# Attention products with V issued for two key steps at a time, seven weight tiles, and the biases loaded later

## The chip, the cores and the metric

One NeuronCore of a Trainium2 chip runs the kernel. The metric is the device time of one execution in microseconds; the time before is the median of three runs. Engines are called PE (TensorE, matrix products), PEld (its weight loads, which overlap PE), DVE (VectorE), ACT (ScalarE), POOL (GpSimd) and SP (the queue that issues the transfers). PSUM has 8 banks of 128 x 512 f32, into which PE writes.

## What is computed

A transformer block on x of 16 x 1024 x 256, f32. Both halves read the layer-normed x, and their results are added to x.

```python
x = L0_attn_x                                     # (16, 1024, 256)
xn = _layernorm(x, axis=-1)
x = x + _L0_attn_ref(xn, ...) + _L0_ffn_ref(xn, ...)

# attention: 16 heads of 16, rotary positions, causal
Q, K, V = x @ Wq.T + bq, x @ Wk.T + bk, x @ Wv.T + bv
scores = einsum('bhqd,bhkd->bhqk', rope(Q), rope(K)) / 4, masked to keys <= query
out = einsum('bhqk,bhkd->bhqd', softmax(scores), V) @ Wo.T + bo

# feed-forward: squared relu, then five steps of a threshold neuron, counted
h = square(relu(x @ W_fc.T)); y = h @ W_proj.T    # 1024 hidden
mem = 0.9 * mem + y - (mem > 1); count += (mem > 1)   # 5 times, count / 5
```

## The kernel before

**Arithmetic.** A full-width product is done as three f16 products of high and low parts (`three`, L599), 128 x 128 weights with 256 or 512 columns. Scores have 16 rows a head, and with the parts of the split they have 48 to 50; two such products lie in the upper and the lower half of the array's rows. The products with V have f32 operands, 17 of 32 columns of the array for each of four heads, so that four lie side by side. The code calls these three layouts of the array FULL, ROWS and COLS.

**Units.** A batch has four units of four heads, 64 units in all. For each unit, `largest` (scores at L797) finds the rows' maxima with DVE (L813, L831), turns them with a small COLS product (L858) and writes them into the operand `qS` by DMA. `weighted` then does the same scores transposed (L914), with the maxima taken off in the product; ACT takes the exponential out of the bank into a tile `w` (L975), 128 keys x 2 heads x 512 queries; POOL zeroes the part past the diagonal (L932); PE multiplies by V (L941) into a bank `pav` in which all key steps of 512 queries add up. There are two blocks of 512 queries; the first has 3 steps of keys, the second 7. A step has four exponentials in two tiles `w`, and one op with its products with V: 4 heads x 1 part, or x 2 parts where two narrow diagonal parts share a step. An f32 product is two instructions in the trace, so a step of one part is 8 matmuls at L941. At the last step, `avT` is copied out and goes through DRAM to be divided by the sums (`av`, `inv`, `ahl`), and `projected` applies Wo.

**Beside it.** `forward` does the feed-forward: `ph` (12 products), relu and squares in a tile `relu`, split into `hT`, then `py` (12 products) and five threshold counts. `norms`, `rotated` (Q and K, bias, rotation in tiles `qk` and `ms`, split into `qkhl`, stored to DRAM `scr_q`, `scr_k`, read back by `load_slots` as `qS`, `kS`) and `values` prepare the next batch. For batch 0, DVE does the rotation; for the others POOL does it.

**Order.** Nothing is ordered by hand. Each piece of work is an `op` with an engine, a cost and a due time; `Plan.order` plays the whole kernel forward with these costs and writes down the order in which each engine starts its ops, and that order is fixed in the program. An op may start at most WINDOW (93 us of the plan's time) before it is due. Tiles come from rings (`BUFS`: the number of buffers for each name), and an op isn't taken until its tiles and banks are free in the plan. Banks are shared out by kind (`CAPS`). PE prefers work in the layout that it is in, and a change costs SWITCH = 100 ns in the plan. In this version the plan's costs are also varied by up to 3%, with a seed for each stretch of 70 us (`DRAWN`, `VARIED`).

**Start.** SP first issues x, Wqkv, cos and sin. `load_small` (L534 to L537, five transfers: Wo in two, bv in two of 128 single elements each, bo) follows, then the transposes of the normed x (L636), which PE's first full products wait for. A small product of bv and Wo (L555) adds the bias of V to bo; x times 5 plus that bias (L1144, L1146) is prepared for each pair of row blocks.

## Time and profile before

| what | value |
|---|---|
| median of 3 runs (lowest to highest) | 2427.77 us (2427.6 to 2428.23) |
| the profiled execution, its own time | 2432.1 us |
| its span, first to last instruction | 2430.4 us |
| DVE busy | 2000.4 us (82%) |
| ACT busy | 1878.6 us (77%) |
| POOL busy | 1769.9 us (73%) |
| exponentials (L975, ACT) | 2560, 1246.4 us |
| products with V (L941, PE) | 6144 matmuls, busy 620.7 us |
| scores (L914 and L797, PE) | 3072 matmuls each, busy 430.5 and 420.6 us |
| full products (L599, PE), the two largest groups | 379.8 and 353.5 us busy |
| mean granted PE clock | 0.992 |

A row of a group gives the line, engine, operation and tile, how many there are, the busy time and the mean duration in ns; a row of the timeline gives its start, how long it lasts until the last of its merged instructions ends, and their number. Matmuls overlap in the pipeline, so their busy time is longer than the distance from start to start, and the starts are what a sum over PE's work goes by. A wait is listed as waiter <- releaser: total us, times, longest.

### The profile page before, as it was taken

To read this page: it belongs to the slowest core of one execution; us is meant where nothing else is said; L and a number is where in the kernel's file an instruction comes from. 1 tells how busy PE (TensorE), PEld (TensorE's weight loads), DVE (VectorE), ACT (ScalarE), POOL (GpSimd) and SP (SyncE) were. 2 spreads that over 40 slices of the span, in tenths; PEclk is the share of its full clock that TensorE was granted. 3 is DMA by queue.
4 is the path that set the end of the run, shared out by engine and by line. 5 is a ranking of instruction groups with operands and counts; after the bars stand their busy time and mean duration, and the time that the engine had idled before them with its cause. 6 is when DMAs were issued, how large, how long until landed. Compare 5 with 4: busy or idle time off the path is not lost. (4 is left out here: it accounts for less than half of the span.)

```text
span 2430.4 us, 58976 instructions
## 1 busy us (share of the span) xinstructions
PE 2344.1 (96%) x20996; PEld 1175.5 (48%) x20996; DVE 2000.4 (82%) x6070; ACT 1878.6 (77%) x3671; POOL 1769.9 (73%) x1897
## 2 busy tenths in 40 slices
PE   4999999999999999999999999999999999999997
PEld 2644444454455444454544445445454444545453
DVE  7788888888978888878888887988878888787982
ACT  5588788877877877878778877777877878778774
POOL 4878778777787787768768687676876858787453
PEclk9999999999999999999999999999999999999998
DMA  7443533524334243244342334333433343433221
GB/s 180 107 104 85 137 85 102 133 80 111 94 106 120 86 120 106 85 107 118 90 120 87 100 115 102 98 91 93 117 92 100 103 108 95 106 107 88 65 59 50
DMA packets 253936, 246.22 MB, mean 101 GB/s; under 512 B 108104, under 2 KB 207816, under 8 KB 253640
## 3 DMA queue, kind: packets, MB, share of 16 engines
q1 hardware_dynamic: 253504, 242.44, 36.4%
q8 instruction: 165, 2.70, 0.5%
q14 instruction: 131, 1.07, 0.2%
q10 hardware_dynamic: 136, 0.00, 0.0%
HBM read 122.82 MB, written 101.71 MB: 92 GB/s over the span
## 5 line engine op out<-in xcount | busy, mean ns | idle before, releaser
L975 ACT ACTIVATE w<-banks 128x512 f32<-128x512 f32 (+1 forms) x2560 | 1246.4, 573 | 285.3 <-PE banks L914 267.3
L813 DVE TENSOR_REDUCE nm_sb<-banks 128x1 f32<-128x512 f32 x1024 | 643.3, 682 | 138.8 <-PE banks L797 134.6
L941 PE MATMUL banks<-w,v_sb 128*32 128x512 f32 (+3 forms) x6144 | 620.7, 495 | 2.4 <-POOL w L932 0.4
L932 POOL TENSOR_SCALAR_AFFINE_SELECT w<-w 128x256 f32<-128x256 f32 x1024 | 398.0, 407 | 287.2 <-ACT w L975 275.1
L831 DVE CUSTOM_DVE_ANT_0 junk<-banks,mask,nm_sb 128x256 bf16<-128x256 f32 (+3 forms) x1024 | 498.7, 546 | 71.6 <-PE banks L797 40.2
L831 DVE CUSTOM_DVE_ANT_0 junk<-banks,mask 128x256 bf16<-128x256 f32 (+3 forms) x1024 | 444.6, 486 | 75.7 <-PE banks L797 60.3
L914 PE MATMUL banks<-qS,kS 50*128 50x512 f16 (+3 forms) x3072 | 430.5, 327 | 12.3 <-DVE nm_sb L831 7.6
L797 PE MATMUL banks<-kS,qS 48*128 48x512 f16 (+3 forms) x3072 | 420.6, 326 | 14.2 <-DVE nm_sb L831 5.4
L599 PE MATMUL banks<-wproj_hi,hT 128*128 128x256 f16 x2048 | 379.8, 274 | 1.1 <-DVE nm_sb L831 0.6
L599 PE MATMUL banks<-xT,wfc_hi 128*128 128x256 f16 x2048 | 353.5, 275 | 6.5 <-ACT qk L679 2.3
L599 PEld LDWEIGHTS <-hT 128*128 128x128 f16 x3072 | 281.0, 98 | 105.3 <-issue 73.7
L1113 POOL TENSOR_TENSOR relu<-relu 128x1024 f32<-128x1024 f32 x111 | 211.1, 1902 | 160.6 <-ACT hT L1111 160.3
L599 PE MATMUL banks<-xT,wfc_lo 128*128 128x256 f16 x1024 | 280.4, 274 | 0.0
L599 PE MATMUL banks<-wproj_lo,hT 128*128 128x256 f16 x1024 | 279.4, 273 | 0.0
L1117 POOL TENSOR_TENSOR hT<-relu,hT 128x1024 f16<-128x1024 f32 x128 | 274.1, 2141 | 3.6 <-ACT relu L1115 1.7
L914 PEld LDWEIGHTS <-kS 50*128 50x128 f16 x3072 | 132.9, 94 | 296.3 <-issue 269.1
L797 PEld LDWEIGHTS <-qS 48*128 48x128 f16 x3072 | 138.7, 94 | 277.7 <-issue 236.1
L941 PEld LDWEIGHTS banks<-w,v_sb 128*32 128x32 f32 x6144 | 151.6, 108 | 250.8 <-issue 195.3
L1128 DVE SCALAR_TENSOR_TENSOR x<-banks,x 128x512 f32<-128x512 f32 x320 | 219.0, 684 | 46.0 <-PE banks L599 39.1
L1106 ACT ACTIVATE relu<-banks 128x512 f32<-128x512 f32 x256 | 156.3, 611 | 121.6 <-PE banks L599 118.2
L599 PEld LDWEIGHTS <-wfc_hi 128*128 128x128 f16 x2048 | 184.6, 98 | 95.2 <-issue 72.7
L686 POOL TENSOR_TENSOR ms<-qk,sin_sb 128x1024 f32<-128x1024 f32 x60 | 142.0, 2367 | 47.6 <-ACT qk L679 47.6
(81 smaller groups left out, 2798.5 us busy)
## 6 DMA issues: line engine op xcount, KB each, us to landing
av_dram<-avT SPq DMA_DIRECT2D x128, 256.0 KB, 2.5
qS<-scr_q SPq DMA_DIRECT2D x128, 192.0 KB, 3.6
kS<-scr_k SPq DMA_DIRECT2D x128, 192.0 KB, 4.4
x<-in_x_dram SPq DMA_DIRECT2D x66, 256.0 KB, 3.7
scr_q<-qkhl SPq DMA_DIRECT2D x32, 512.0 KB, 3.1
scr_k<-qkhl SPq DMA_DIRECT2D x32, 512.0 KB, 3.1
av<-av_dram SPq DMA_DIRECT2D x64, 256.0 KB, 3.4
inv<-inv SPq DMA_DIRECT2D x64, 256.0 KB, 3.4
```

The costliest lines, as they stand in the source:

```text
L599: nc.tensor.matmul(out, lhsT=lhs[i], rhs=rhs[j], start=first and n == 0, stop=last and n == 2)
L797: nc.tensor.matmul(pts[two].t[:, at : at + w], lhsT=qS.t[r, h, c * P : (c + 1) * P], rhs=kS[r, h, k0 : k0 + w], start=True, stop=True,)
L813: lambda two=two, pt=pt: nc.vector.tensor_reduce(nm0[:, two, i, c : c + 1], pt.t, axis=AX.X, op=ALU.max),
L831: nc.vector.tensor_tensor_reduce(next(junk)[:, :w], pt.t[:, at : at + w], mask[:, QB - w :], scale=1.0, scalar=nm0[:, two, i, chunk] if pa ...
L914: nc.tensor.matmul(pts[two].t[:, at : at + n], lhsT=kS[r, i, j * P : (j + 1) * P], rhs=qS.t[r, i, qb * QB + off : (qb + 1) * QB], start=Tr ...
L932: nc.gpsimd.affine_select(out=d, in_=d, compare_op=ALU.is_ge, fill=0.0, base=0, pattern=[[0, 2], [1, P]], channel_multiplier=-1,)
L941: nc.tensor.matmul(pav.t[VT * h : VT * (h + 1), off:], lhsT=st.v[:, j, col : col + VT], rhs=ws[h % 2].t[:, h // 2, at : at + QB - off], st ...
L975: lambda n=n, two=two, pt=pt, w=w: nc.scalar.activation(w.t[:, two, :n], pt.t[:, :n], AF.Exp, scale=SCALE),
L1106: lambda r=r, ph=ph, pr=pr: nc.scalar.activation(r.t[:, 2 * pr : 2 * pr + 2].rearrange("p f t -> p (f t)"), ph.t, AF.Relu, scale=1.0 / WS),
L1113: combined(1024, when + 4e3, lambda e, r=r: e.tensor_tensor(r.t, r.t, r.t, ALU.mult), [], [(r, 0), (r, 1)], 1.75, lambda r=r: nc.scalar.ac ...
L1117: lambda e, r=r, hT=hT: e.tensor_tensor(hT.t[:, 1], r.t, hT.t[:, 0], ALU.subtract),
L1128: nc.vector.scalar_tensor_tensor(xc, py.t, WS * LEAST[step], xc, ALU.is_gt, ALU.add)
```

## The change

The products with V are collected (`given`) and issued as one op for two steps of keys (JOINED = 2), or for what is left at the last step of a block of queries. The ring `w` has seven tiles instead of five; for the space, `x` has eight instead of nine and `ahl` five instead of six, and the rotation's tile `ms` has no ring of its own any more but takes a buffer of the two in the ring `relu`. The due time of a product is 12 us after its step instead of 8 (LAG). `load_small` is due at 32 us of the plan's time instead of -20 us, and the loads of x for batch 0's result may not start much before it. The variation of the plan's costs is gone.

```diff
-LAG = 8e3
+LAG = 12e3
-BUFS = dict(w=5, xn=2, x=9, relu=2, hT=3, avT=2, ahl=6)
+BUFS = dict(w=7, xn=2, x=8, relu=2, hT=3, avT=2, ahl=5)
+JOINED = 2
-SMALL = -20e3
+SMALL = 32e3
-VARIED, STRETCH = 0.03, BATCH / 2
-DRAWN = [
...
-                    cost *= varied.uniform(1 - VARIED, 1 + VARIED)
...
-    op("sp", dma(5), SMALL, load_small, [], ["small", wo_stage], size=1400.0, window=10e3)
+    op("sp", 5e3, SMALL, load_small, [], ["small", wo_stage], size=1400.0, window=10e3)
...
-                ms = held("ms", 1, [P, 2, QB], F32, f"ms_{b}_{t}_{half}")
+                ms = held("relu", 2, [P, 2, QB], F32, f"ms_{b}_{t}_{half}")
...
-        def product(pav, ws, parts, first, last):
-            for n, (qb, j, off, at) in enumerate(parts):
+        def product(pav, given, first, last):
+
+            todo = [(ws, part) for ws, parts in given for part in parts]
+            for n, (ws, (qb, j, off, at)) in enumerate(todo):
                 for h in range(4):
...
-                        start=first and n == 0, stop=last and n == len(parts) - 1,
+                        start=first and n == 0, stop=last and n == len(todo) - 1,
...
-                pav = bank(f"pav_{unit}_{qb}")
+                pav, given, begun = bank(f"pav_{unit}_{qb}"), [], True
...
-            op("pe", pe(n, 4) + 20 * len(parts), when + LAG,
-               lambda pav=pav, ws=ws, parts=parts, first=first, last=last: product(
-                   pav, ws, parts, first, last),
...
+            given = given + [(ws, parts)]
+            if len(given) == JOINED or last:
+                all_parts = [part for _, parts in given for part in parts]
+                op("pe", sum(pe(QB - part[2], 4) + 20 for part in all_parts), when + LAG,
+                   lambda pav=pav, given=given, begun=begun, last=last: product(pav, given, begun, last),
+                   [*[(w, two) for ws, _ in given for w in ws for two in range(2)],
+                    *[(key, st.b % 2, part[1] // 2) for part in all_parts for key in ("v", "v taken")]],
+                   [pav], mode=COLS)
+                given, begun = [], False
...
-                        st.x[t - 1] = x_ = load_x(b, t - 1, "x", times[0] - 15e3)
+                        st.x[t - 1] = x_ = load_x(
+                            b, t - 1, "x", times[0] - 15e3,
+                            min(WINDOW, times[0] - 5e3 - SMALL) if b == 0 else None)
```

More of the change, by code (lines that the diff above doesn't have):

```diff
@@ L3 @@
 from itertools import cycle
-from random import Random
 import numpy as np
@@ L219, in order @@
         mode = None
-        drawn, change, varied = list(DRAWN), -1e9, None
         def turn(t, need):
@@ L273, in order @@
             now = events[0][0]
-            if now >= change:
-                varied = Random(drawn.pop(0) if drawn else 0)
-                change = S0 + STRETCH if change < S0 else change + STRETCH
             while events and events[0][0] <= now:
@@ L424, in held, with load_x @@
         return Held(sb, tag, BUFS.get(tag, bufs), shape, dtype, name)
-    def load_x(b, n, tag, when):
+    def load_x(b, n, tag, when, window=None):
         t = held(tag, 0, [P, 2, D], F32, f"{tag}_{b}_{n}")
         op("sp", 500, when, lambda: nc.sync.dma_start(t.t, tokens(x, b, n)), [], [t],
-           size=move(P * 2 * D * 4))
+           size=move(P * 2 * D * 4), window=window)
         return t
@@ L981, in weighted @@
                        [(w, 0), (w, 1)])
-            op("pe", pe(n, 4) + 20 * len(parts), when + LAG,
-               lambda pav=pav, ws=ws, parts=parts, first=first, last=last: product(
-                   pav, ws, parts, first, last),
-               [*[(w, two) for w in ws for two in range(2)], *[(key, st.b % 2, part[1] // 2) for part in parts for key in ("v", "v taken")]], [pav], mode=COLS)
+            given = given + [(ws, parts)]
[7 more added lines that the diff above has]
+                given, begun = [], False
             if last:
```

2 lines of the change are left out of this document (removed).

## Prediction

> **What bounds the kernel now.** I read the busy shares first, then the waits, then the timeline of PE.
>
> ```profile
> PE 2344.1 (96%) x20996; PEld 1175.5 (48%) x20996; DVE 2000.4 (82%) x6070; ACT 1878.6 (77%) x3671; POOL 1769.9 (73%) x1897
> ```
>
> PE is the bound, and it is idle for little. The list of waits agrees: ACT and POOL wait for hundreds of us, PE's longest entries are a few us each.
>
> ```profile
> ACT w L975 <- PE banks L914: 267.3, 288, 4.0
> PE banks L599 <- ACT qk L679: 8.5, 3, 6.2
> PE banks L914 <- DVE nm_sb L831: 7.6, 13, 3.1
> ```
>
> So time comes off only where PE's own steps get shorter or its small waits do. What a step costs stands in PE's timeline, in the starts. Three cuts from it: a lone step of products with V, a doubled one (which this order already has in places), and a change between full and row layout.
>
> ```profile
> 412.02 0.60 PE L914 MATMUL banks<-qS,kS 50*128 50x512 f16 x4
> 412.56 1.06 PE L941 MATMUL banks<-w,v_sb 128*32 128x512 f32 x8
> 413.56 0.39 PE L797 MATMUL banks<-kS,qS 48*128 48x512 f16 x2
> ...
> 878.20 0.60 PE L797 MATMUL banks<-kS,qS 48*128 48x384 f16 x6
> 878.73 1.92 PE L941 MATMUL banks<-w,v_sb 128*32 128x512 f32 x16
> 880.59 0.61 PE L914 MATMUL banks<-qS,kS 50*128 50x512 f16 x4
> ...
> 401.68 0.27 PE L599 MATMUL banks<-wo_lo,ahl 128*128 128x256 f16 x1
> 401.78 0.27 PE L599 MATMUL banks<-wo_hi,ahl 128*128 128x256 f16 x1
> 401.99 0.39 PE L914 MATMUL banks<-qS,kS 50*128 50x384 f16 x4
> 402.22 0.38 PE L797 MATMUL banks<-kS,qS 48*128 48x512 f16 x2
> ```
>
> From the start of L941 to the next scores, 8 matmuls take 413.56 - 412.56 = 1.00 us and 16 take 880.59 - 878.73 = 1.86, so a second step costs 0.86 and entering and leaving the layout the rest. With the way in (scores to L941 takes 0.31 as the median of the trace, scores to scores 0.22) a lone excursion costs 0.31 + 1.00 - 0.22 = 1.09; less the 0.86 of its work, 0.23 us go to two changes of layout, 0.11 each. Full to row is 401.99 - 401.78 = 0.21 where full to full is 0.10 to 0.11: 0.10 for that change.
>
> **Joined products: the sum.** In the built order, 640 products with V become 384 ops; runs of PE's order in one layout fall from 2367 to 2053, so 314 changes are saved. The column layout is entered 358 times instead of 578, full against row changes rise from 1210 to 1336. That is 440 changes saved at 0.11 (48 us) less 126 added at 0.10 (13 us): -35 us. More exactly, I gave every succession of two PE steps its median start-to-start gap in the trace and added these along both orders: 2277.6 us before, 2244.8 after. **I take -33 us**; the count of changes alone bounds it at -30 to -36. It lies on the path, PE's own queue.
>
> From its first to its last matmul PE takes 2402.3 us, so 124.7 us are waits and the slower clock: 23 up to 125 us, 82 up to 2385, 19 in the tail. These can grow.
>
> **Joined products: the waits.** An op waits for eight exponentials and their masks instead of four, and holds four of seven tiles `w` meanwhile (two of five before). Behind it in PE's queue stand scores, and ACT waits for those. I added the same medians of the PE work that stands between the last scores of a step and its product: in the worst tenth 2.07 us before, 2.06 after. Between a bank's scores and its next use, for scores after exponentials: 1.31 before and 1.62 after. The cover is no thinner, so I take the middle stretch at -4 us, pro rata to 6% fewer PE ops; bounds: -10, and +15, a fifth more waits, if the order made from unvaried costs meets ACT and DVE less well.
>
> **Two bare stretches.** The new order has two places without full products between the attention steps, where PE can only follow ACT. The row for such a place is the last stretch before:
>
> ```profile
> 2385.00:2409.00 24.00, 21.98 (x177) 8.42 (x174) 3.81 (x6) 18.61 (x41) 8.71 (x18) 0.93 0.13 36
> ...
> L975 ACT ACTIVATE w<-banks 128x512 f32<-128x512 f32 (+1 forms) x38 | 17.6, 575 | 4.1 <-PE banks L914 4.1
> ```
>
> (Columns: stretch, length, PE, PEld, DVE, ACT, POOL, granted clock, DMA share, GB/s.) 38 exponentials in 24 us are 0.63 us each; ACT's own work bounds it below at 17.6/38 = 0.46.
> First, the tail: the last `py` now ends 33 us of PE work before the end, with 66 exponentials to go (18 us and 37 before). 66 x 0.46 = 30 to 66 x 0.63 = 42 us against 27.5 us of PE work up to the last projection: +3 to +14, less the 6 that the old tail loses by the same count. I take +5, bounds -3 to +9. The chain after it (store, sums, `inv`, `ahl`, projection) is the same.
> Second, near 300 us, where batch 3 is prepared: 23 us of PE work with 44 exponentials and two `pv`, no `ph`, no `py`. Its four `ms` now take the two `relu` buffers in turn, each held through three POOL passes of 2.37, 2.37 and 2.55 us, and `ph` can't start without one. ACT's other work there is 10 us (3 `qkhl`, 2 `qk`, 2 `avT`, the norm of four row blocks, by their rows 3.2 + 1.4 + 1.2 + 3.9). 44 x 0.46 + 10 is 30 us, 44 x 0.63 is 28 without it and 38 with it: +5 to +15; **I take +9**.
> The clock: 0.93 over 24 us is 1.7 us lost there, so +2 for the two (0 to +5).
>
> [...]
>
> **Seven tiles, rings, costs.** The tiles change no instruction. x at eight and `ahl` at five have rings that the order was built with; the projection's cover over its `ahl` stays 39 us in the middle (40 before). Seven relu squares move from ACT to POOL, 7 x 1.9 = 13 us on an engine busy 73%. Nothing, covered by PE; uncovered at most 13, as far as it falls in the bare stretch and is counted there.
>
> **The biases.** Before, SP issues them ahead of the first transpose:
>
> ```profile
> 8.79 0.60 SPq L534 DMA_DIRECT2D wo_stage<-in_wo_dram  x1
> ...
> 15.89 0.54 SPq L535 DMA_DIRECT2D bv_sb<-in_bv_dram  x1
> 19.55 0.35 SPq L537 DMA_DIRECT2D bo_sb<-in_bo_dram  x1
> ...
> 21.53 1.37 SPq L636 DMA_TRANSPOSE xT<-xhl  x1
> ```
>
> The normed tile that it turns is done at 14.6 us (DVE L658), so PE's first full product, 4.1 us behind the transpose at 25.6, can start at 18.7: 6.9 us sooner. But PE's first scores wait for batch 0's keys, which come through DVE's rotation, a store and a load:
>
> ```profile
> PE banks L797 <- DMA kS<-scr_k: 1.5, 1, 1.5
> ```
>
> They start at 79.9, 13.2 us after DVE's last rotation op ended (66.7), 54.3 us behind the first full product; 37.9 of those are PE work. In the new order 30.5 us of PE work stand there, and DVE has 1.7 us more in the chain (the bias ops). So scores start at 18.7 + 54.3 + 1.7 = 74.7, with 7.4 us less work done: 5.2 sooner by the clock, 2.2 lost by the work. The five transfers stand now ahead of the first store of Q, which waits for DVE until about 40; they need 12.7 us from about 26 on and are covered. Not covered, they would delay that store. I take 0; bounds -7 (the chain isn't late) and +3.
>
> **Sum.** 2430.4 - 33 - 4 + 5 + 9 + 2 + 0 = 2409 us of span. The profiled execution has 1.7 us around its span and stands 4.3 over the median, so its span is 2.6 over: 2409 - 2.6 = **2406 us**.
>
> **The rivals.**
> - *The bare stretches cost nothing and the early start is kept.* For it: ACT is busy only 77%, and it could run at its 0.46 there. Against: the row of 0.63. 2427.8 - 33 - 4 - 7 = 2384.
> - *No change.* Joined waits eat the saving: 384 ops, each late by 0.09 us, make 33. For it: PE's weight loads wait for POOL's masks in 79 places already (28 us). Against: the covers above. 2427.
> - *Slower: the shared ring.* `ms` and `relu` meet in every batch, not only where the order shows a bare stretch; if `ph` is late on the chip at each preparation, a stretch like the one at 300 us stands in the others too. At 9 us each it decides from the fourth on (4 x 9 > 33). With six: 2406 + 5 x 9 = 2451. For it: POOL waits up to 13 us for ACT at L1113, so the relu chain is often late. Against: the order has full products between the scores everywhere else, and each `relu` is 25 us ahead of its `py`.
> - *It doesn't join*, because the order doubled products already: excluded by the 358 against 578 runs.
>
> **Chances.** Forecast 0.62, first rival 0.20, no change 0.08, slower 0.10. A measurement here tells 0.2%, 5 us, from no change. Faster: 0.82, same 0.08, slower 0.10. The bounds of the unknown costs seldom all fall one way; their distances from the values taken, squared and added, give -13 to +21, so 2393 to 2427 for the forecast alone. The range reaches down to 2384 for the first rival and ends at 2426; left out are the slower case, half of no change and some 0.06 of the first rival, 0.2 in all.
>
> **What would show it.** Right: L941's runs of 8 mostly gone in PE's timeline and a lone excursion again at 1.00; PE's first full product near 18.7 us; scores' wait for `kS` of several us where 1.5 stood; PE idle near 300 us and in a tail of about 40 us behind the last `py`; PE's busy time lower by about the overlap of the changes. Wrong: PE waits on `w` all through, POOL masks as releasers of L941 grown beyond 28 us, or bare stretches at other batches.

## The result, and the profile after

The changed kernel takes 2446.79 us (median of 6 runs, 2442.22 to 2456.57), the kernel before 2428.0 beside it (6 runs, 2426.13 to 2433.61). The ratio is 1.0074, with a 95% interval of 1.0058 to 1.009: slower by 19 us, where 2406 was forecast. The profiled execution took 2446.82 us, its span is 2445.1. The one before, of 2430.4, stood 4 us over its median, so the two spans differ by 14.7 only. Line numbers are 8 to 10 lower than before: full-layout products are L589, scores for the maxima L787, scores for the exponentials L904, products with V L933, exponentials L967, the reductions of the maxima L803 and L821.

The busy shares of the page, which the prediction read first:

```profile
PE 2328.7 (95%) x20996; PEld 1205.1 (49%) x20996; DVE 1985.7 (81%) x6068; ACT 1866.8 (76%) x3666; POOL 1782.0 (73%) x1904
```

PE does the same 20996 matmuls and is busy 15.4 us less, and yet the span is 14.7 us longer: what PE saved, and as much again, has become waiting. PE's timeline says that its steps are what the change wanted (columns: start, us from the first start to the last end, engine, line, operation, tiles, shape, count):

```profile
999.67 1.04 PE L933 MATMUL banks<-w,v_sb 128*32 128x512 f32 x8
1000.64 0.39 PE L787 MATMUL banks<-kS,qS 48*128 48x512 f16 x2
...
1003.56 1.93 PE L933 MATMUL banks<-w,v_sb 128*32 128x512 f32 x16
1005.42 0.61 PE L787 MATMUL banks<-kS,qS 48*128 48x512 f16 x6
```

A lone step takes 1000.64 - 999.67 = 0.97 us to the next start (1.00 before), a joined one 1005.42 - 1003.56 = 1.86 (1.86). The list of waits (engine and line, what it waited for; us in total, times, longest):

```profile
ACT w L967 <- PE banks L904: 226.6, 236, 3.2
...
ACT avT L396 <- PE banks L933: 121.9, 76, 4.5
...
PE banks L589 <- DMA xT<-xhl: 21.9, 2, 19.1
PE banks L589 <- DVE nm_sb L821: 11.5, 32, 1.0
...
PE banks L904 <- DVE nm_sb L821: 8.6, 22, 1.3
PE banks L787 <- DVE nm_sb L821: 7.7, 20, 0.9
PE banks L589 <- ACT qk L669: 6.1, 6, 4.7
```

The third line is PE's start: its first full product now stands at 19.09 us. The lines with `nm_sb` are PE waiting for a bank that VectorE's maxima still hold: L589, L904 and L787 together 27.8 us in 74 times. The same three entries before (the one of L914 stands in the prediction) sum to 16.6 us in 39:

```profile
PE banks L797 <- DVE nm_sb L831: 5.4, 13, 1.8
PE banks L599 <- DVE nm_sb L831: 3.6, 13, 0.4
```

SP's queue, for the biases:

```profile
14.81 1.36 SPq L626 DMA_TRANSPOSE xT<-xhl  x1
...
27.77 0.62 SPq L524 DMA_DIRECT2D wo_stage<-in_wo_dram  x1
28.45 0.58 SPq L525 DMA_DIRECT2D bv_sb<-in_bv_dram  x1
```

The first transpose stands at 14.81 (21.53 before), the biases behind it. Now the two stretches without full-layout products, by windows (columns as in the prediction; the eighth figure, before the DMA share, is the granted clock):

```profile
352.00:397.00 45.00, 39.76 (x301) 14.61 (x299) 33.62 (x116) 32.71 (x69) 37.09 (x42) 0.85 0.40 111
...
2370.00:2385.00 15.00, 12.56 (x110) 3.98 (x110) 14.93 (x43) 10.21 (x20) 2.84 (x3) 1.00 0.10 37
...
2385.00:2400.00 15.00, 12.93 (x78) 3.79 (x80) 1.49 (x6) 9.80 (x24) 6.09 (x15) 0.70 0.06 20
2400.00:2415.00 15.00, 12.60 (x70) 2.86 (x62) 0.35 (x1) 9.52 (x19) 0.81 (x2) 0.73 0.17 55
```

Before, the first stretch of the tail was

```profile
2360.00:2385.00 25.00, 24.25 (x224) 12.18 (x223) 16.77 (x48) 18.84 (x37) 14.20 (x15) 1.00 0.10 34
```

The tail now has two halves. Up to 2385 VectorE is busy 14.93 of 15 us (16.77 of 25 before), most of it with the maxima: they bound it. Behind that no engine is busy throughout: PE is busy 12.93 and 12.60 of 15, ScalarE 9.80 and 9.52, at a granted clock of 0.70 and 0.73 (0.93 in the tail before). In the rows of the timeline a bracket gives the idle time before and what ended it. One turn of it, from the timeline:

```profile
2402.05 5.01 ACT L967 ACTIVATE w<-banks 128x512 f32<-128x512 f32 x10
...
2405.67 3.06 PE L933 MATMUL banks<-w,v_sb 128*32 128x512 f32 x16
...
2408.66 0.61 PE L904 MATMUL banks<-qS,kS 50*128 50x512 f16 x4
2409.15 3.04 ACT L967 ACTIVATE w<-banks 128x512 f32<-128x512 f32 x6 [2.08 <-PE banks L904]
```

A joined product that took 1.93 us in the middle takes 3.06 here. ScalarE runs out of filled score banks meanwhile and idles for 2.08 us, until PE has issued scores again.

Laid out as in the prediction, for three kernels (the last is the first experiment below). "PE sum" is the sum of the median gaps of before along each order; "excess" is what PE's starts took beyond it, in waits and at half clock.

| us | before | changed | changed, products single |
|---|---|---|---|
| first matmul | 23.75 | 19.09 | 17.72 |
| PE sum | 2277.6 | 2244.8 | 2280.1 |
| excess up to 125 us | 23.4 | 27.8 | 27.5 |
| excess 350 to 400 us | 2.0 | 17.7 | 6.5 |
| excess from 2340 us | 20.5 | 39.8 | 21.9 |
| excess elsewhere | 78.9 | 91.6 | 85.2 |
| behind the last matmul's start | 4.3 | 4.3 | 4.1 |
| span | 2430.4 | 2445.1 | 2443.0 |

The PE sum fell by 32.8 us and the start came 4.7 earlier; 52.1 us of excess took the place of these.

### The profile page after: what moved, and what is told of

It is laid out like the page before. It is cut to its first block, busy times and chain, and to the rows that moved or that the text cites. A ratio compares the mean times of both kernels' runs of the same rounds, so it can differ in the third digit from the quotient of the medians.

```text
span 2445.1 us, 58685 instructions
## 1 busy us (share of the span) xinstructions
PE 2328.7 (95%) x20996; PEld 1205.1 (49%) x20996; DVE 1985.7 (81%) x6068; ACT 1866.8 (76%) x3666; POOL 1782.0 (73%) x1904
## 4 chain that ended last, share of the span: by engine, by line
PE 62%; DVE 19%; ACT 7%; issue 5%; DMA 4%; POOL 3%; SPq 1%; DVEq 0%; POOLq 0%; ACTq 0%
PE banks L589 29%; PE banks L933 16%; PE banks L904 9%; PE banks L787 8%; DVE junk L821 7%; DVE nm_sb L803 5%; ACT w L967 5%; DVE x L1125 3%; DVE nm_sb L821 1%; DVE stats L606 1%; PE banks L848 1%; DMA x<-in_x_dram 1%; DMA qS<-rows 1%; DMA inv<-inv 1%; DMA xn<-in_x_dram 1%
## 5 line engine op out<-in xcount | busy, mean ns | idle before, releaser
L967 ACT ACTIVATE w<-banks 128x512 f32<-128x512 f32 (+1 forms) x2560 | 1248.5, 578 | 245.8 <-PE banks L904 226.6
L803 DVE TENSOR_REDUCE nm_sb<-banks 128x1 f32<-128x512 f32 x1024 | 641.2, 682 | 149.0 <-PE banks L787 148.1
L821 DVE CUSTOM_DVE_ANT_0 junk<-banks,mask,nm_sb 128x256 bf16<-128x256 f32 (+3 forms) x1024 | 498.1, 546 | 98.8 <-PE banks L787 67.6
L933 PE MATMUL banks<-w,v_sb 128*32 128x512 f32 (+3 forms) x6144 | 569.8, 499 | 6.6 <-DVE nm_sb L803 2.0
L821 DVE CUSTOM_DVE_ANT_0 junk<-banks,mask 128x256 bf16<-128x256 f32 (+3 forms) x1024 | 445.6, 486 | 82.7 <-PE banks L787 64.7
L904 PE MATMUL banks<-qS,kS 50*128 50x512 f16 (+3 forms) x3072 | 437.8, 328 | 21.5 <-DVE nm_sb L821 8.6
L787 PE MATMUL banks<-kS,qS 48*128 48x512 f16 (+3 forms) x3072 | 411.8, 326 | 13.6 <-DVE nm_sb L821 7.7
L589 PE MATMUL banks<-wproj_hi,hT 128*128 128x256 f16 x2048 | 380.3, 274 | 3.9 <-DVE nm_sb L821 2.8
L589 PE MATMUL banks<-xT,wfc_hi 128*128 128x256 f16 x2048 | 352.0, 274 | 16.1 <-DVE nm_sb L821 4.8
L589 PEld LDWEIGHTS <-hT 128*128 128x128 f16 x3072 | 282.2, 98 | 107.1 <-issue 76.0
L933 PEld LDWEIGHTS banks<-w,v_sb 128*32 128x32 f32 x6144 | 172.3, 111 | 316.8 <-issue 258.9
L1110 POOL TENSOR_TENSOR relu<-relu 128x1024 f32<-128x1024 f32 x118 | 223.5, 1894 | 122.1 <-ACT hT L1108 122.0
L589 PE MATMUL banks<-wproj_lo,hT 128*128 128x256 f16 x1024 | 279.8, 273 | 0.0
L589 PE MATMUL banks<-xT,wfc_lo 128*128 128x256 f16 x1024 | 279.8, 273 | 0.0
L904 PEld LDWEIGHTS <-kS 50*128 50x128 f16 x3072 | 133.5, 94 | 261.4 <-issue 231.3
L787 PEld LDWEIGHTS <-qS 48*128 48x128 f16 x3072 | 139.4, 94 | 221.2 <-issue 172.5
L589 PEld LDWEIGHTS <-wfc_hi 128*128 128x128 f16 x2048 | 186.0, 98 | 105.7 <-issue 85.0
L1125 DVE SCALAR_TENSOR_TENSOR x<-banks,x 128x512 f32<-128x512 f32 x320 | 217.8, 681 | 23.4 <-PE banks L589 16.5
L821 DVE DVE_READ_ACCUMULATOR2_ANT nm_sb<- 128x1 f32 x2048 | 168.7, 82 | 0.0
```

What stands on the lines that cost most here:

```text
L589: nc.tensor.matmul(out, lhsT=lhs[i], rhs=rhs[j], start=first and n == 0, stop=last and n == 2)
L787: nc.tensor.matmul(pts[two].t[:, at : at + w], lhsT=qS.t[r, h, c * P : (c + 1) * P], rhs=kS[r, h, k0 : k0 + w], start=True, stop=True,)
L803: lambda two=two, pt=pt: nc.vector.tensor_reduce(nm0[:, two, i, c : c + 1], pt.t, axis=AX.X, op=ALU.max),
L821: nc.vector.tensor_tensor_reduce(next(junk)[:, :w], pt.t[:, at : at + w], mask[:, QB - w :], scale=1.0, scalar=nm0[:, two, i, chunk] if pa ...
L904: nc.tensor.matmul(pts[two].t[:, at : at + n], lhsT=kS[r, i, j * P : (j + 1) * P], rhs=qS.t[r, i, qb * QB + off : (qb + 1) * QB], start=Tr ...
L933: nc.tensor.matmul(pav.t[VT * h : VT * (h + 1), off:], lhsT=st.v[:, j, col : col + VT], rhs=ws[h % 2].t[:, h // 2, at : at + QB - off], st ...
```

## The experiments

Three theories went in. *Bare stretches*: where no full-layout product is left to put between the attention's steps, PE waits for ScalarE and VectorE and its clock falls (0.70 and 0.73 above). *Joining costs everywhere*. *The other edits*, the shared ring of `ms` and `relu` above all. Each time is the median of at least four runs, each ratio is to runs of the kernel before on the same chip (2427.3 to 2430.1 us in the five sets); "stretches" are those of over 6 us of PE work without a full-layout product in its built order. The excess is that of the one profiled execution, which can stand some us off the median (**other_draw** 4.1 over it, **joined_draw2** 4.6 under it).

| kernel | products with V | stretches, us | PE sum | excess | median us | ratio to before (95%) |
|---|---|---|---|---|---|---|
| before | single | 9.2 | 2277.6 | 124.8 | 2428.0 | |
| changed | joined | 13.6, 26.5 | 2244.8 | 176.9 | 2446.8 | 1.0074 (1.0058 to 1.009) |
| single | single | 13.2 | 2280.1 | 141.1 | 2446.2 | 1.0073 (1.0061 to 1.0086) |
| small_as_before | joined | 6.4, 15.2 | 2247.4 | 162.5 | 2438.0 | 1.0033 (1.002 to 1.0046) |
| var1 | joined | 13.0, 12.4 | 2244.6 | 170.9 | 2436.9 | 1.0033 (1.002 to 1.0045) |
| w6 | joined | 15.0, 38.8 | 2244.0 | 199.4 | 2466.6 | 1.0157 (1.0136 to 1.0179) |
| rings_only | single | 9.2 | 2279.6 | 136.2 | 2445.2 | 1.0066 (1.0052 to 1.008) |
| rings_joined | joined | 6.6, 15.2 | 2244.7 | 159.9 | 2434.0 | 1.0021 (1.0011 to 1.0031) |
| rings_joined_not_last | joined but 2 units | 13.8 | 2246.0 | 152.3 | 2426.8 | 0.9992 (0.9984 to 1.0001) |
| joined_own_ms | joined | 15.5, 10.8, 49.5 | 2242.0 | 204.1 | 2471.5 | 1.0177 (1.0163 to 1.0191) |
| no_variation | single | 11.6 | 2275.9 | 133.4 | 2436.6 | 1.004 (1.0028 to 1.0052) |
| other_draw | single | 9.2 | 2277.5 | 144.8 | 2445.5 | 1.0073 (1.006 to 1.0086) |
| ms_shared_only | single | none | 2279.5 | 152.0 | 2460.4 | 1.0134 (1.0121 to 1.0147) |
| filled_tail | joined | 13.6, 14.6 | 2255.8 | 166.0 | 2444.5 | 1.0072 (1.0059 to 1.0085) |
| rings_only_draw2 | single | 9.2 | 2275.4 | 133.4 | 2438.7 | 1.0034 (1.0022 to 1.0047) |
| joined_draw2 | joined | 15.4 | 2245.0 | 153.4 | 2431.6 | 1.0006 (0.9995 to 1.0016) |
| not_last_draw2 | joined but 2 units | 13.8 | 2246.0 | 145.9 | 2421.9 | 0.9973 (0.9963 to 0.9984) |
| not_last_long_stretch | joined but 2 units | 42.6 | 2249.4 | 161.3 | 2439.7 | 1.004 (1.0027 to 1.0053) |
| draw2_oldest_bank | joined but 2 units | 13.8 | 2246.0 | 148.0 | 2421.7 | 0.9961 (0.9949 to 0.9973) |
| before_oldest_bank | single | 9.2 | 2277.6 | 117.0 | 2422.1 | 0.9959 (0.9946 to 0.9973) |

### What undoing one edit gives

**single** takes the joining alone back:

```diff
-JOINED = 2
+JOINED = 1
```

> The changed kernel with JOINED = 1: every step's product with V is issued by itself again; the other edits stay (seven weight tiles, biases behind the first transposes, ms in the relu buffers, LAG of 12 us, no variation of the planned durations). In its built order the longest run of PE work without a full-layout product is 13.2 us, at the end (9.2 us in the kernel before, 13.6 and 26.5 us in the changed kernel); the stretch near 300 us is gone. By the gaps from before its PE sum is 2.5 us over that of the kernel before. Theory 'bare stretches' (a stretch without full-layout products costs about 1.17 us for each us of its PE work: 36 us of excess for 31 us of such work): 2430.4 + 2.5 + 4.7 for the 4.0 us more of stretch, less 4.7 for the earlier start, so about 2433 against a profile of 2430 before, a ratio of 0.999 to 1.004. Rival 'joining costs everywhere' (the whole excess of 52 us comes with joined products, wherever they stand): the excess goes and the early start stays, about 2427, ratio 0.997 to 1.000. Rival 'the other edits' (rings, biases, the order without variation carry the excess): 52 us of excess without the 33 us won, 2475 and over, ratio above 1.015.

Measured 2446.2 us, 1.0073. All three missed: joining is worth nothing here, neither the 33 us of its PE sum nor a loss. The table above says where it went. Against this kernel the changed one has 35.3 us less PE sum and 35.8 us more excess: 11.2 at 350 to 400 us, 17.9 from 2340 us, 6.4 elsewhere and 0.3 at the start. And this kernel, in which nothing is joined, has lost 16.3 us of excess against before all the same.

**small_as_before** puts the biases back ahead of the first transposes:

```diff
-SMALL = 32e3
+SMALL = -20e3
-    op("sp", 5e3, SMALL, load_small, [], ["small", wo_stage], size=1400.0, window=10e3)
+    op("sp", dma(5), SMALL, load_small, [], ["small", wo_stage], size=1400.0, window=10e3)
```

(and `load_x` gets no window of its own for batch 0.)

> The changed kernel with the loads of the biases and of wo put back where they stood (SMALL and its planned cost and window as before); products stay joined. In its built order the stretch near 300 us is gone and the last one falls into two of 6.4 and 15.2 us of PE work; the PE sum by the gaps from before is 30.2 us under the kernel before's. Theory 'bare stretches': 21.6 us of them against 9.2, so +14.5; no early start; the excess of the middle stays at +9: 2430.4 - 30.2 + 14.5 + 9 = 2424, ratio to before 0.995 to 1.000. Rival 'joining costs everywhere': the 52 us stay, 2452, ratio 1.005 to 1.011. Rival 'the other edits': as the changed kernel or better by what the biases carry, which would show near the start and not at 352 to 397 us or behind 2385.

Measured 2438.0. The excess of 350 to 400 us is 2.9 (17.7), that from 2340 us 31.2 (39.8), as the stretches of the built order are gone or shorter; but 14 us more than the theory's sum are lost.

**var1** draws the planned durations within 3% again:

```diff
+        varied = Random(1)
...
+                    cost *= varied.uniform(0.97, 1.03)
                     heappush(events, (now + cost, n, 1, o))
```

> The changed kernel with every planned duration drawn within 3 per cent again (one seed for the whole plan), which changes nothing but the order. Stretches without full-layout products in its built order: 13.0 us near 296 us and 12.4 us at the end (26.5 in the changed kernel); PE sum by the gaps from before 33.0 under the kernel before's. Theory 'bare stretches': 25.4 against 9.2, +19: 2430.4 - 33 - 4.7 + 19 + 9 = 2421, ratio 0.993 to 0.999, and the tail behind 2385 us about 14 us shorter than in the changed kernel, at a higher granted clock. Rival 'joining costs everywhere': no difference from the changed kernel, ratio 1.005 to 1.010.

Measured 2436.9. The excess from 2340 us fell to 30.2, that at 350 to 400 stayed at 16.6, as its stretches say; again 16 us more than the sum.

**w6** takes a weight tile away: `w=6` in `BUFS`.

> The changed kernel with six weight tiles in place of seven. Stretches without full-layout products in its built order: 15.0 us near 292 us and 38.8 us at the end; PE sum by the gaps from before 33.6 under the kernel before's. Theory 'bare stretches': 53.8 against 9.2, +52: 2430.4 - 33.6 - 4.7 + 52 + 9 = 2453, ratio 1.008 to 1.014, slower than the changed kernel, with the loss of 14 us behind 2385 us and a lower granted clock there. Rival 'joining costs everywhere, through the weight tiles that a joined product holds': one tile fewer to pass costs in every batch, in the middle of the run, so the middle's excess (+9 in the changed kernel) at least doubles and the tail doesn't change. Rival 'the number of tiles and the tail are of no account': same as the changed kernel, 1.006 to 1.009.

Measured 2466.6, the tail's excess 52.8 (39.8) with its longer stretch. The middle's excess didn't double (98.8 elsewhere, 91.6). So the stretches order the four joined kernels rightly (**small_as_before** and **var1**, with 21.6 and 25.4 us of them, stand level), and every sum, that of **single** too, is 13 to 16 us short. These had to come from something that all of them share.

### From before, one edit at a time

**rings_only** is the kernel before with `BUFS = dict(w=7, xn=2, x=8, relu=2, hT=3, avT=2, ahl=5)` and `ms` held under `relu`; **rings_joined** joins its products; **rings_joined_not_last** joins them but for the last two of 64 units:

```diff
-            if len(given) == JOINED or last:
+            if len(given) == (JOINED if unit < 62 else 1) or last:
```

**joined_own_ms** is the kernel before with `JOINED = 2`, `w=6`, `x=8`, `ahl=5`, `ms` in its own buffer.

> The kernel before with the tile edits alone: seven weight tiles, eight tiles of x, five of ahl, ms in the two relu buffers. No joining; the biases, LAG and the variation of the planned durations as before. In its built order the longest stretch without full-layout products is 9.2 us, as before; PE sum by the gaps from before 2279.6 (2277.6 before). The runs so far put the excess over the PE sum at 125 to 141 us where products are single (9 and 13 us of stretch). Theory 'bare stretches': 23.3 + 2279.6 + 125 + 4.3 for what follows the last matmul, so 2432, ratio 0.999 to 1.003. Rival 'shared ring' (relu and ms starve each other in every batch): the 16 us that the kernel with single products lost against before come from here, 2446, ratio 1.005 to 1.008.

> The same with the products joined: all of the change but the biases, LAG and the dropped variation. Stretches without full-layout products in its built order: 6.6 and 15.2 us of PE work, both at the end, none near 300 us; PE sum by the gaps from before 2244.7. Theory 'bare stretches' as the first runs size it (joined: excess 138 us and 1.15 us for each us of stretch): 23.3 + 2244.7 + 138 + 25 + 4.3 = 2435, ratio 1.000 to 1.004. Rival 'the other edits' (biases, LAG and variation carry what was lost, joining earns its 33 us): 23.3 + 2244.7 + 125 + 4.3 = 2397, ratio 0.987. Rival 'joining costs everywhere': no better than the changed kernel, ratio 1.006 to 1.009.

> The same with the products of the last two of the 64 units issued singly, the other 62 joined. Stretch in its built order: 13.8 us at the end (6.6 and 15.2 before this edit); PE sum 2246.0. Theory 'bare stretches', with the mechanism that a joined product (3 to 4 us) outlasts the four score banks that ScalarE still has (about 2 us), so that PE and ScalarE take turns where ScalarE is the bound: ScalarE's gaps of over 1.5 us behind 2385 us go, and the excess there falls from about 30 us to the 20 of the kernels with single products: 8 to 10 us faster than the kernel above, about 2426, ratio 0.997 to 1.000. Rival 'granted clock alone' (a stretch without full products halves the clock, whatever its products): 1 us less per us of stretch, 8 us, but ScalarE's gaps stay. Rival 'joining in the middle': no difference, within 3 us of the kernel above.

> The kernel before with the products joined, ms still in a buffer of its own, and so six weight tiles (eight of x, five of ahl); the biases, LAG and the variation as before. The plan then has no full products left much sooner at the end: stretches of 15.5, 10.8 and 49.5 us of PE work behind 2150 us of PE work; PE sum 2242.0, the lowest of all. Theory 'bare stretches': 23.3 + 2242 + 138 + 1.15 x 76 + 4.3 = 2495, ratio 1.022 to 1.032, the slowest, and all of it behind about 2290 us. Rival 'shared ring': the ring is gone, so is the loss, 2400, ratio 0.987 to 0.993. Rival 'joining costs everywhere': the changed kernel's excess of 177 us, 2447, ratio 1.005 to 1.010.

The tile edits alone lose 16 us (2445.2 against 2428.7 beside it). Joining then gains 11 us (2434.0), and 24 of its 35 us come back as excess. Leaving the last two units single gains another 7.2 us (2426.8), a little under the 8 to 10 expected of the turns. The two orders are the same in the first 20548 of 20996 matmuls, up to 2352 us, so this gain is the tail's. In these kernels full products are L601, scores for the exponentials L916, products with V L945, exponentials L979 and the maxima's reductions L833. The timeline of the tail of **rings_joined**:

```profile
2399.90 3.18 PE L945 MATMUL banks<-w,v_sb 128*32 128x512 f32 x16
2403.01 1.00 PE L916 MATMUL banks<-qS,kS 50*128 50x384 f16 x8
2403.71 3.17 ACT L979 ACTIVATE w<-banks 128x512 f32<-128x512 f32 x8 [2.20 <-PE banks L916]
```

and that of **rings_joined_not_last**:

```profile
2394.73 6.66 ACT L979 ACTIVATE w<-banks 128x512 f32<-128x512 f32 x15
2395.72 1.03 PE L916 MATMUL banks<-qS,kS 50*128 50x512 f16 x4
2396.68 1.06 PE L945 MATMUL banks<-w,v_sb 128*32 128x512 f32 x8
```

With joined products ScalarE idles for 2.20 us behind one; with single ones it runs 15 exponentials without a gap, 6.66/15 = 0.44 us each. By its 3.18 us (1.93 for the one at 2395.14 in the same tail) the joined product shown ran at half clock for most of its time, and the single one (1.06, 1.04 in the middle of the changed kernel) didn't, but that isn't the whole of it: from 2340 us to the last exponential 10.2 us stood at half clock with joined products and 6.8 with single ones, which is worth at most 1.7 us, while ScalarE's idle times of over 1 us sum to 15.1 and 9.1 us there. They didn't all go: one of 1.90 us is left behind 2385. **joined_own_ms** has no shared ring and the lowest PE sum, and is the slowest of all: against the shared ring as the cause, and for the stretches, though its 76 us of them cost less than 1.15 us each (2471.5 in place of 2495).

### The order before is a good draw

Why does a kernel in which nothing is joined lose 16 us? The order of before comes from 34 drawn seeds. **no_variation** sets `VARIED` to 0, **other_draw** changes the seeds and nothing else, **ms_shared_only** moves `ms` to `relu` alone:

```diff
-                varied = Random(drawn.pop(0) if drawn else 0)
+                varied = Random(8 + (drawn.pop(0) if drawn else 0))
```

> The kernel before with the variation of the planned durations at nothing; nothing else is edited, so only the order is another. PE sum by the gaps from before 2275.9 (2277.6 before), longest stretch without full-layout products 11.6 us (9.2). The tile edits alone cost 16 us without a stretch that explains them. Theory 'redrawn order' (the order of the kernel before is a good draw, which any edit loses, whatever it edits): the excess is that of the other kernels with single products, 136 to 141 in place of 125: 23.5 + 2275.9 + 138 + 4.3 = 2442, ratio 1.003 to 1.007. Rival 'the tile edits': the excess stays at 125 to 128, 2430, ratio 0.998 to 1.002.

> The kernel before with other random numbers for the same variation (each seed 8 higher); nothing else is edited. PE sum 2277.5, longest stretch 9.2 us, both as before to 0.1. Theory 'redrawn order': 23.5 + 2277.5 + 138 + 4.3 = 2443, ratio 1.003 to 1.007. Rival 'the tile edits': as before, ratio 0.998 to 1.002.

> The kernel before with one edit: ms takes the two relu buffers; five weight tiles, nine of x, six of ahl, as before. PE sum 2279.5, no stretch over 6 us in the built order. Theory 'shared ring' (the products for hT wait for buffers that ms holds, in every batch): the 16 us of the tile edits come from here, ratio 1.005 to 1.008. Theory 'redrawn order': 1.003 to 1.007 as well, so this run tells the two apart only with the two above: where they are at 1.000 and this one is not, it is the ring. Rival 'fewer tiles of x and ahl': ratio 0.998 to 1.002, all three.

**other_draw** computes the same with the same tiles, has a PE sum within 0.1 us and the same stretch, and takes 2445.5: the whole loss of the change, from a draw. **no_variation** loses 9 us. So what **rings_only** and **single** lost needs no cause in their edits. **ms_shared_only** loses 33 us, outside every range given for it and nearly twice the most that another draw with single products lost; whether that is the ring or a poor draw one kernel can't say, but **rings_only** has the same ring.

### What joining is worth within a draw

The three kernels under a second draw (each seed 16 higher), and a fourth under a draw whose order runs out of full products early (160 higher):

> The kernel with the tile edits alone (products single), with other random numbers for the variation of the planned durations (each seed 16 higher). PE sum by the gaps from before 2275.4 (2279.6 with the first numbers), longest stretch without full-layout products 9.2 us (9.2). Theory 'a draw is worth as much as the change' (what a kernel loses outside the stretches is set by the draw of its order, and the kernel before has a good one): the excess of the five other kernels with single products, 133 to 152, gives 23 + 2275.4 + 141 + 4.3 = 2444, ratio 1.002 to 1.010. Rival 'the tile edits themselves cost': the 11 us of excess of the first draw again, 2439, and no other draw of the tile edits would be under 1.004; so a ratio under 1.002 speaks for the draw, over 1.004 for either.

> The same random numbers with the products joined. PE sum 2245.0, 30.4 under the kernel above; one stretch of 15.4 us at the end (9.2 above). Theory: with the first random numbers joining took 34.9 us from the PE sum and 11 us from the time; 24 us came back as waits, about 8 of them in the tail. The same here: 2434, 8 to 14 us faster than the kernel above. Rival 'the order's draw alone' (joining is worth nothing, the 11 us were luck): no difference to the kernel above beyond 3 us. Rival 'joining earns its PE sum where the tail is short': 25 us faster than the kernel above.

> The same random numbers, products joined but for the last two of the 64 units. PE sum 2246.0, stretch 13.8 us at the end. Theory 'taking turns' (with the first random numbers 7 us less than all joined): 6 to 9 us faster than the kernel above, 2427, ratio 0.997 to 1.001. Rival 'luck of the draw': within 3 us of the kernel above.

> The same kernel, last two units single, with a draw (each seed 160 higher) whose order runs out of full-layout products early: a stretch of 42.6 us of PE work at the end, all of it with single products; PE sum 2249.4, 3.4 over the draws above. It asks what a stretch costs without joined products in it. Theory 'granted clock' (without full products the clock falls to half for part of the time, 20 of 37 us in the changed kernel, joined or not): 29 us more of stretch at a quarter to a half of their length, 7 to 14 us, and the 3.4: 2437 to 2445, ratio 1.004 to 1.008, with half clock in a third or more of the 45 us before the last projections. Theory 'taking turns alone' (only joined products make ScalarE idle): the clock stays up, only the 3.4, 2430, ratio 0.999 to 1.003.

2438.7, 2431.6, 2421.9: joining gains 7 us, leaving the last two units single another 10, as under the first draw (11 and 7). The second step is again the tail's: the orders are the same in the first 20548 matmuls, 6.8 us stand at half clock in both from 2340 us to the last exponential, and ScalarE's idle times of over 1 us there fall from 12.6 to 8.0 us. The first step is less sure. The same seeds don't give the same order, joined and single orders part at some 122 us, and kernels with single products alone range from 2422 to 2460 us; so two gains of 7 and 11 us are likely joining's own, and not shown to be. **not_last_draw2** is faster than both kernels of this case (0.9973 to before). What was given back in the middle stands in the list of waits. In **rings_only_draw2**:

```profile
PE banks L601 <- DVE nm_sb L833: 5.8, 18, 0.5
```

in **joined_draw2**:

```profile
PE banks L601 <- DVE nm_sb L833: 21.4, 57, 1.0
```

Full-layout products wait 16 us more for banks that VectorE's maxima hold (15.5 in 43 against 4.7 in 17 under the first draw, 11 us more). This doesn't hang on the draw: over all kernels here the entry is 3.6 to 8.5 us in the eight with single products and 11.4 to 25.9 in the twelve with joined ones. The windows of **not_last_long_stretch**:

```profile
2345.00:2385.00 40.00, 33.53 (x266) 10.17 (x264) 36.74 (x120) 28.75 (x59) 11.62 (x21) 0.96 0.14 43
2385.00:2415.00 30.00, 26.38 (x197) 7.52 (x194) 3.57 (x11) 23.79 (x52) 10.00 (x24) 0.89 0.13 38
```

It lost 15 us from 2340 us on against the first draw (41.0 against 26.1), within what the clock was to cost, but not by the clock: only 10 us there stood at half clock. In the first 40 us VectorE is busy 36.74 us (30.23 in the same 40 us of the kernel before): the maxima bound it. So a stretch costs without joined products too, and neither theory had named the engine.

### The clock, tried with added work

**filled_tail** adds full-layout matmuls in the last unit of the changed kernel:

```diff
+            if unit >= 63:
+                for i in range(4):
+                    pw = bank(f"pw_{unit}_{qb}_{parts[0][1]}_{i}")
+                    op("pe", pe(QB), when + LAG,
+                       lambda pw=pw: nc.tensor.matmul(
+                           pw.t, lhsT=w_proj[0][:, 0, :P], rhs=w_proj[0][:, :2, :],
+                           start=True, stop=True),
+                       [(ws[i // 2], i % 2), *WPROJ], [pw])
```

> The changed kernel with 40 full-layout matmuls of 512 columns added in the last of the 64 units, four for each step, each behind one exponential, into a free bank that nothing reads (work left over, the outputs are the same). They are 40 x 0.215 = 8.6 us of PE work and with their layout changes 11.0 us of PE sum; the last stretch without full-layout products shrinks from 26.5 to 14.6 us. Theory 'granted clock': of the 37 us behind 2387 us until the last exponentials, in which the changed kernel had 20 us at half clock, less than 8 us stay at half clock, some 6 to 10 us come back, and the added work costs little beyond: 2446 to 2452, ratio 1.007 to 1.010. Theory 'taking turns alone' (PE and ScalarE wait for each other, the clock follows from that and does no harm of its own): nothing comes back, 2452 to 2458, ratio 1.010 to 1.013, at whatever clock. Rival 'the clock falls for the whole end, whatever runs': the half clock stays at about 20 us.

Its windows:

```profile
2385.00:2400.00 15.00, 12.48 (x107) 4.05 (x100) 3.60 (x11) 10.97 (x25) 6.45 (x16) 1.00 0.06 20
2400.00:2415.00 15.00, 14.65 (x109) 4.29 (x100) 0.35 (x1) 11.88 (x25) 2.44 (x5) 1.00 0.17 55
```

and a joined product among the added ones (L978):

```profile
2404.20 0.87 PE L978 MATMUL banks<-wproj_hi 128*128 128x512 f16 x2
2405.00 0.39 PE L904 MATMUL banks<-qS,kS 50*128 50x512 f16 x2
2405.32 1.92 PE L933 MATMUL banks<-w,v_sb 128*32 128x512 f32 x16
```

The clock is 1.00 where it was 0.70 and 0.73, the 16 matmuls take 1.92 us again, and the kernel with 11 us more PE sum takes 2444.5 us, 1.0072 against the changed kernel's 1.0074. From 2340 to 2424 us one piece of 3.4 us at half clock is left, at 2378, ahead of these windows; the changed kernel had 20.4 us. PE's listed waits between 2385 and 2424 us were 4.3 us in the changed kernel and are 3.9 here: they can't have covered 11 us. What paid for most of them is work that no longer runs at half clock, by its size (20.4 - 3.4)/2 = 8.5 us; the rest is within the 2.4 us by which this execution's first matmul came earlier.

### Which bank

**draw2_oldest_bank** and **before_oldest_bank** keep the order of all of PE's instructions and take the bank that has been free longest:

```diff
-                        t.at = banks.index(True)
+                        t.at = min((i for i in range(BANKS) if banks[i]), key=lambda i: since[i])
```

> The fastest kernel so far (products joined but for the last two units, second random numbers) with one edit: a bank is taken from among those that have been free longest, and not the first free one by number. The order of all instructions is the same on PE; only the bank numbers differ. It asks whether the waits of full-layout products for a bank that VectorE's score maxima still hold (21.2 us in 57 waits in that kernel, 21.4 in 57 with all products joined, 5.8 in 18 with single products under the same numbers) come from scarcity or from the choice of the bank. Theory 'scarcity' (joined products make longer stretches of scores, which fill all eight banks; in the plan 518 of the 576 products with a bank of their own get the only free one): these waits stay at 15 to 22 us, and the time falls by no more than the waits of scores for banks, 0 to 6 us: 2416 to 2422. Rival 'choice': they fall under 8 us, the time by 13 or more, 2409.

> The kernel before with the same edit of the choice of banks, its order of instructions unchanged. Full-layout products wait 3.6 us in 13 waits for banks of VectorE's maxima there, scores 13 us. Theory 'scarcity': 0 to 6 us off, 2422 to 2428. Rival 'choice': the same, as there is little to gain. Rival 'the good draw of the kernel before was one of banks too' (another choice loses what the other draws lost): 2436 or over.

The wait in question, in **draw2_oldest_bank**:

```profile
PE banks L601 <- DVE nm_sb L833: 25.9, 68, 1.0
```

It didn't fall (21.2 in 57 times without the edit) and even stands above the 15 to 22 expected: the banks are scarce, not badly chosen. The time stayed too (2421.7). But the kernel before gained 8 us from the edit (0.9959), more than expected of either, with waits between scores falling from 29.1 to 16.6 us of excess. So the best version with joined products and the best with single ones stand level, 0.9961 and 0.9959, though under different draws.

## Why the prediction was wrong

The sum was -33 -4 +5 +9 +2 +0 = -21 us of span; +14.7 came. By the table it is made of -32.8 (PE sum), -4.7 + 4.4 (start), +12.7 (middle), +8.9 (near 350 us), +12.5 (tail) and +13.6 (clock, at most). By its steps:

- **Joined products, the sum: right.** The -32.8 is the prediction's own sum, the gaps of before laid along the new order. The trace of the changed kernel bears it out: in the middle of the run the median gaps of the commonest successions (full to full, full to row, row to full, row to column) are those of before within 0.002 us. The prices of 0.11 and 0.10 us per change hold.
- **The waits in the middle, -4: wrong, +12.7.** The step that failed is "The cover is no thinner". The covers were counts of PE work between a step and what needs it. They don't see who holds the banks: a full product then waits for a maximum to be read. Joining's part of it is shown under two draws (11 and 16 us in that one wait) and by the ranges over all kernels. That longer runs of scores fill the banks fits this (5.6 matmuls in a run of scores before, 6.2 after, on average) and is argued; about half of the 12.7 (6.3, by the table) is in **single** as well and belongs to the draw.
- **The clock, +2: wrong by 12.** In 352 to 397 us 13.6 us stood at half clock, in 2385 to 2424 us 20.4, against 6.8 in the tail before (two pieces, up to 2414 us): (13.6 + 20.4 - 6.8)/2 = 13.6 us, if PE had work in all of it, so at most. The step took the 0.93 of a stretch that was short before and still had some full products in it; in the new tail the clock is 0.70 and 0.73. How far it falls isn't set by the length alone: **not_last_long_stretch**, without full products from 2345 to 2415 us, keeps 0.96 and 0.89. **filled_tail** shows that the added work mends the clock (20.4 us at half clock became 3.4), hardly the listed waits (4.3 and 3.9 us).
- **The tail, +5: wrong, +12.5 without the clock** (39.8 - 20.5 = 19.3 less 20.4/2 - 6.8/2 = 6.8), above its bound of 9. It priced ScalarE's exponentials alone. The tail's first part is VectorE's, 14.93 of 15 us busy, and in its second ScalarE idles behind each joined product. That last part is shown by the two pairs that differ in the tail alone (7 and 10 us).
- **The stretch near 300 us, +9: the size right** (17.7 - 2.0 - 6.8 of clock = 8.9), **the cause wrong.** `ms` in the two `relu` buffers was blamed. **small_as_before**, **rings_joined** and **joined_draw2** have the same ring, and 2.9, 2.4 and 1.8 us there. All three load the biases early; all joined kernels that load them late (changed, var1, w6, filled_tail) have 16.6 us or more. How loads at 28 us come to shape the order near 350 us stays open.
- **Seven tiles, rings, costs, "Nothing": wrong.** Dropping the variation was counted there, and the order of before was taken as a neutral base. A new draw alone costs 9 to 18 us (**no_variation**, **other_draw**), and every edit draws anew. **single**, which has every edit but the joining, takes 2446.2 us against 2429.0 beside it: 17 of the 19 us lost stand there already, about what a draw costs. The 33 us were counted from a base that no edited kernel starts from.
- **The biases, 0: right by itself.** The first matmul came 4.7 us sooner and 4.4 of it were gone by 125 us. Undoing the edit gains 9 us (**small_as_before**), through the order, and no more than one draw is worth.

Of the rivals, the shared ring was to make it slower, at 2451. The time came near that and the mechanism didn't show: the middle has no further stretch like the one at 350 us, and **joined_own_ms** without the ring is slower still. "No change: joined waits eat the saving" named the right thing and not its places. The ways to lose were each bounded by themselves, as if they were independent, and the clock, the tail and the middle all came out high together. A common cause is likely, that longer runs of one layout leave each engine less to put between; that is argued here and not shown.

## What to carry to other kernels

A price per step, read from the bound engine's timeline, can be exact to a per cent and still say little of the time: ask what the engine will wait for once its steps are shorter (here banks, VectorE, ScalarE), and price a stretch without filler by the engine that bounds it and at the clock such a stretch has (0.70 and 0.73 in the changed kernel's tail, 0.96 and 0.89 in **not_last_long_stretch**). Join small steps where the engine that issues them is the bound, and leave them single where another is: the same edit likely gained in the middle, and it lost in the tail. Where an order comes from a planner with drawn numbers, draw the base anew a few times before any comparison; here one draw more or less was worth 9 to 18 us, as much as the change.

## What the runs showed of the hardware

In the changed kernel's tail the granted clock fell to half with only short waits listed for PE. From 2385 to 2424 us all of them are these:

```profile
PE banks L904 <- ACT w L967: 3.6, 10, 0.7
PE banks L848 <- DVE nm_sb L821: 0.5, 1, 0.5
PE banks L904 <- ACT avT L396: 0.2, 1, 0.2
```

None is over 0.7 us, and still 20.4 of the 39 us stood at half clock, in pieces of 3.4 and 6.8 us. Up to 2421.8 us PE was issuing only scores (50 of 128 rows, two at a time) and products in the column layout (32 columns, four at a time) there; 40 full-layout matmuls put between them, 8.6 us of work at 0.215 us from one start to the next (a full-layout matmul of 512 columns in the trace before), came with a clock of 1.00 from 2385 to 2415 us (**filled_tail**). Neither the layout alone nor the listed small waits alone set the clock in these kernels: **not_last_long_stretch** issued no full product for 70 us and had 10.2 us at half clock, where the changed kernel had 20.4 in 52 us; and **filled_tail** has 3.9 us of such waits in the same 39 us, at full clock. What the clock answers to, these runs don't say.

And which of several free banks a tile gets, with the order of instructions unchanged, was worth 8 us in the kernel before (2422.1 against 2430.1) and nothing in the other kernel (2421.7 and 2421.9).
